# Attention block ends spread out and moved to GpSimd, clustering fold by fold: one layer pair on one core

## Chip, core and metric

The kernel runs on one core of one Trainium2 chip. The metric is the device time of one execution in microseconds (us); before the change the median of three runs is 4209.58 us, and they lie between 4209.54 and 4209.81.

The core's engines are named as in the profile: PE (TensorE, matrix products, and PEld its weight loads), DVE (VectorE), ACT (ScalarE), POOL (GpSimd), and SP, which issues the transfers.

## What is computed

Four images x of 256 channels by 64 x 64 points (4096 points) pass through two layers, all in 32-bit floats. The reference, cut to what matters:

```
# layer 0: attention over the 4096 points of an image
q = wq x + bq; k = wk x + bk                  # 32 channels each
attn = softmax(q^T k)                         # 4096 x 4096
v = wv x + bv                                 # 256 channels
x = gamma * (v attn^T) + x
# layer 1: clustering, then an MLP
n = group_norm(x)
feat = f_w n + f_b; val = v_w n + v_b         # 96 channels = 4 heads x 24
# each head, and each of the 2 x 2 folds of the picture (32 x 32 points):
cen, v_cen = 2 x 2 pooled feat, val           # 4 centres
sim = sigmoid(beta + alpha * <norm(cen), norm(feat)>)
sim = sim * one_hot(argmax over centres)
agg = (sim val + v_cen) / (count + 1)
out = sim^T agg                               # back to the points
y = x + ls1 * (proj_w out + proj_b)
y = y + ls2 * (w2 gelu(w1 group_norm(y)))
z = relu(bn(y * dw)); z = relu(bn(pw_w z))
```

## The kernel before

The images are worked on one after the other. An image's x stays in four SBUF tiles of 128 x 2 x 1024 (channels in two halves c, 1024 points each) and is overwritten in place by the attention's result, the clustering's and the MLP's. The order of the instructions on each engine is set by a scheduler from the program order and the buffers' release; a pool of n buffers makes the n+1st tile wait for the first one's last reader.

**Attention** (`attention`). Keys for all 4096 points and 16 pairs of value blocks (`v_pair`, L236) come first, together with the first scores. The 4096 query points form eight blocks (`nb`, 512 points each), and each block meets the keys in eight groups (`g`, 512 keys each): 64 units u. `score` (L266) computes a unit's scores into two PSUM halves (`halves`, two buffers in all), copies them into an SBUF slot `s` on ScalarE, and on VectorE takes the running maximum `top` (L286 from half 1, L289 from half 0). Scores run `LEAD` = 9 units ahead of their use, with 10 slots. When a block's eight units are scored, `fold`, `across` and `spread` make its maximum `mb`; `exps` (L318) then subtracts it on VectorE (L326), takes the exponential on ScalarE (L329) and sums the slots into `acc` on GpSimd (L331, L334), for all units whose turn the scheduler finds. `weigh` (L336) accumulates v times the exponentials into `av` (two PSUM banks, four quarters of a unit, 16 passes on TensorE). A block ends in `finish` (L347): `av` times gamma into `ts`, the denominator `den` (a product of ones with both halves of `acc`), its reciprocal `rden` (L356), a product (L358), the addition of the scaled v bias `gbv` and of x in one instruction (L360), and the statistics for the next norm (L363, `bn_stats`). `acc` has one buffer, so the next block's first sum waits for `den`.

**Clustering** (`cluster`). The first norm, `feat` and `val` (L436, L448), then squares on GpSimd (L504), point norms `nrm` and products with the centres `dots` (L510). `sg` holds the similarities of 128 points by 32 chunks by 16 (head, centre) pairs; `oh` is the one-hot choice. The four folds q are laid side by side in strips of 32: `sim` and `sgp` (with the pooling weights added) are 128 x 8 x 4 x 32, so that `agg` (L565) is computed in strips of 32 output partitions, `g` holds the projected centres of the four folds in four strips of 32 partitions (row 16 of each strip carries proj_b, through `projb` and `row16`), and the output product `op` (L626) uses 32-row strips into four banks. One VectorE instruction per piece then adds ls1 times it into x (L638), and `bn_stats` follows (L646).

**MLP** (`mlp`). The second norm, two matrix products with gelu between, and the last 1x1 convolution; its small tiles `hs` and `o` share the pool tag "w", as do `ts` and `sg`.

At the start, `projb` is made by two small products `pb_p` (L165) that need the transfer `pc_s`; they stand ahead of the first keys on TensorE. SP issues the transfers in program order, x's eight pieces first, then wv_s, bv_s, pc_s and the rest.

Of the kernel before, what the change touches and what calls it, by code (L numbers as in the profile page):

```python
# [8 lines left out]
F32 = mybir.dt.float32  # L9
# [4 lines left out]
P = 128  # L14
# [31 lines left out]
def attention_then_cluster_block(  # L46
# [61 lines left out]
    bv_s = loaded("bv_s", bv.rearrange("(k p o) -> p k o", p=P, o=1), [P, KC, 1])  # L108
# [52 lines left out]

    projb = const.tile([1, C], F32, name="projb")
    pb_p = ps_m.tile([P, NB], F32, tag="m", name="pb_p")
    for k in range(KC):
        nc.tensor.matmul(  # L165
            pb_p[:1, k * P : (k + 1) * P], par("proj_b", k), ident, start=True, stop=True
        )
    nc.vector.tensor_copy(projb, pb_p[:1, :C])
    row16 = const.tile([1, 4, 32], F32, name="row16")
    nc.gpsimd.memset(row16, 0.0)  # L170
    nc.gpsimd.memset(row16[:, :, 16:17], 1.0)

    gbv = const.tile([P, KC], F32, name="gbv")
    nc.vector.tensor_scalar(
        gbv, bv_s.rearrange("p k o -> p (k o)"), pv_s[:, PV["gamma"] : PV["gamma"] + 1], None, ALU.mult
    )
# [33 lines left out]
    def attention(b, xs):  # L210
# [25 lines left out]
        def v_pair(i):  # L236
            ps = ps_m.tile([P, 2, C], F32, tag="m", name=f"vp_{b}_{i}")
            for j in range(2):
                o = ((2 * i + j) * P) % XT
                for k in range(KC):  # L240
                    nc.tensor.matmul(  # L241
                        ps[:, j, :],
                        xs[(2 * i + j) * P // XT][:, k, o : o + P],
                        wv_s[:, k, :],
                        start=(k == 0),
                        stop=(k == KC - 1),
                    )
            if i % 2:
                nc.scalar.copy(v_t[:, 2 * i : 2 * i + 2, :], ps)
            else:  # L250
                nc.vector.tensor_copy(v_t[:, 2 * i : 2 * i + 2, :], ps)
# [44 lines left out]
        def across(nb):  # L296
            top = tops.pop(nb)
            tp = ps_m.tile([P, 4, P], F32, tag="m", name=f"tt_{b}_{nb}")
            for j in range(4):
                nc.tensor.transpose(tp[:, j, :], top[:, 0, j * P : (j + 1) * P], ident)  # L300
            mx = small.tile([P, 4], F32, tag="mx", name=f"mx_{b}_{nb}")
            nc.vector.tensor_reduce(mx, tp, AX.X, ALU.max)
            dg = work.tile([P, 4, P], F32, tag="dg", bufs=1, name=f"dg_{b}_{nb}")
            nc.vector.tensor_tensor(
                dg,
                ident.unsqueeze(1).to_broadcast([P, 4, P]),
                mx.unsqueeze(2).to_broadcast([P, 4, P]),
                ALU.mult,
            )
            return dg  # L310
# [36 lines left out]
        def finish(nb, av):  # L347
            acc = accs.pop(nb)
            ts = [work.tile([P, NB], F32, tag="w", bufs=5, name=f"t_{b}_{nb}_{c}") for c in range(KC)]
            nc.scalar.activation(ts[0], av[0], AF.Identity, scale=pvc("gamma"))  # L350
            nc.vector.tensor_scalar(ts[1], av[1], pvc("gamma"), None, ALU.mult)
            den = ps_m.tile([P, NB], F32, tag="m", name=f"den_{b}_{nb}")
            for t in range(2):
                nc.tensor.matmul(den, ones, acc[:, t, :], start=(t == 0), stop=(t == 1))
            rden = work.tile([P, NB], F32, tag="rden", bufs=1, name=f"rden_{b}_{nb}")
            nc.vector.reciprocal(rden, den)  # L356
            for c in range(KC):
                nc.vector.tensor_tensor(ts[c], ts[c], rden, ALU.mult)  # L358
                yb = block(xs, c, nb)
                nc.vector.scalar_tensor_tensor(  # L360
                    yb, ts[c], gbv[:, c : c + 1], yb, ALU.add, ALU.add
                )
                nc.vector.bn_stats(stats[:, 2 * nb + c, :], yb)  # L363
# [18 lines left out]
        av = None  # L382
        for u in range(units):
# [17 lines left out]
            weigh(u, av, 1)  # L401
            weigh(u, av, 2)
# [5 lines left out]
            if g == GRP - 1:  # L408
                finish(nb, av)
# [7 lines left out]
    def cluster(b, ys, stats):  # L417
# [99 lines left out]
        prn = work.tile([P, P], F32, tag="q", name=f"prn_{b}")  # L517
# [8 lines left out]
        sg = work.tile([P, NB], F32, tag="w", bufs=5, name=f"sg_{b}")  # L526
# [14 lines left out]
        nc.vector.tensor_tensor(quad(oh), quad(oh), over_m(best), ALU.is_equal)  # L541

        sim = spool.tile([P, 8, 4, 32], F32, tag="s", name=f"sim_{b}")
        sgp = spool.tile([P, 8, 4, 32], F32, tag="s", name=f"sgp_{b}")
        nc.gpsimd.memset(sim[:, :, :, 16:], 0.0)
        nc.gpsimd.memset(sim[:, :, :, 16:17], 1.0)
        nc.gpsimd.memset(sgp[:, :, :, 16:], 0.0)

        def folded(t):
            return t.rearrange("p (q j s) -> p q j s", q=4, j=8)  # L550

        for q in range(4):
            nc.vector.tensor_tensor(
                sim[:, :, q, :16], folded(sg)[:, q], folded(oh)[:, q], ALU.mult
            )

            nc.vector.tensor_tensor(
                sgp[:, :, q, :16], sim[:, :, q, :16], folded(pool_w)[:, q], ALU.add
            )


        agg_p = ps_m.tile([P, NB], F32, tag="m", name=f"agg_{b}")
        for j in range(8):
            for q in range(4):
                nc.tensor.matmul(  # L565
                    agg_p[q * 32 : (q + 1) * 32, :ED],
                    sgp[:, j, q, :],
                    val[q // 2][:, q % 2, j, :],
                    start=(j == 0),
                    stop=(j == 7),  # L570
                )
        cnt_p = ps_m.tile([P, NB], F32, tag="m", name=f"cnt_{b}")
        nc.tensor.matmul(cnt_p[:ED], ones[:, :ED], oh, start=True, stop=True)
        sums = work.tile([P, ED], F32, tag="q", name=f"sums_{b}")
        nc.scalar.copy(sums, agg_p[:, :ED])
# [12 lines left out]
        aggt = ps_m.tile([P, NB], F32, tag="m", name=f"aggt_{b}")  # L588
        nc.tensor.transpose(aggt[:ED, :P], sums, ident)
        agg = work.tile([P, 4, 32], F32, tag="q", name=f"aggs_{b}")  # L590
        nc.gpsimd.memset(agg, 0.0)
        nc.vector.tensor_tensor(
            agg[:ED, :, :16],
            aggt[:ED, :P].rearrange("p (q s) -> p q s", q=4)[:, :, :16],
            rc[:ED].rearrange("p (q s) -> p q s", q=4),
            ALU.mult,
        )

        gp = ps_m.tile([P, NB], F32, tag="m", name=f"gp_{b}")
        nc.tensor.matmul(  # L600
            gp[:, :C], agg[:ED].rearrange("p q s -> p (q s)"), wproj_s, start=True, stop=False
        )
        nc.tensor.matmul(gp[:, :C], row16.rearrange("p q s -> p (q s)"), projb, start=False, stop=True)
        g_s = work.tile([P, C], F32, tag="acc", bufs=1, name=f"g_{b}")
        nc.scalar.copy(g_s, gp[:, :C])

        sim_t = spool.tile([P, 2, NB], F32, tag="s", name=f"simt_{b}")
        for hb in range(2):
            tp = ps_m.tile([P, NB], F32, tag="m", name=f"tp_{b}_{hb}")
            for j in range(4):  # L610
                nc.tensor.transpose(
                    tp[:, j * P : (j + 1) * P],
                    sim[:, 4 * hb + j].rearrange("p q s -> p (q s)"),
                    ident,
                )
            nc.scalar.copy(sim_t[:, hb], tp)
        stats2 = small.tile([P, 2 * NBLK, 6], F32, tag="stats", name=f"st2_{b}")
        for hb in range(2):
            for c in range(KC):
                ops = [  # L620
                    ps_s.tile([P, 2, NB], F32, tag="s", name=f"op_{b}_{hb}_{c}_{f}")
                    for f in range(2)
                ]
                for q in range(4):
                    rows = slice(q * 32, (q + 1) * 32)
                    nc.tensor.matmul(  # L626
                        ops[q // 2][:, q % 2, :],
                        g_s[rows, c * P : (c + 1) * P],
                        sim_t[rows, hb, :],
                        start=True,  # L630
                        stop=True,
                    )
                for q in range(4):
                    fh, fw = q // 2, q % 2
# [3 lines left out]
                    nc.vector.scalar_tensor_tensor(  # L638
                        yq,
                        ops[fh][:, fw, :].rearrange("p (h w) -> p h w", h=16),  # L640
                        par("ls1", c),
                        yq,
                        ALU.mult,
                        ALU.add,
# [5 lines left out]
    def mlp(b, ys, stats2):  # L650
        ga, gb = group_norm(b, "gn2", stats2)
        ob = out[b].rearrange("(k p) h w -> p k (h w)", p=P)
        for nb in range(NBLK):
# [25 lines left out]
            for j in range(HID // P):  # L679
# [9 lines left out]
                h_s = work.tile([P, NB], F32, tag="w", bufs=5, name=f"hs_{b}_{nb}_{j}")  # L689
# [16 lines left out]
            for c in range(KC):  # L706
# [9 lines left out]
                o_s = work.tile([P, NB], F32, tag="w", bufs=5, name=f"o_{b}_{nb}_{c}")  # L716
# [88 lines left out]
```

## Time and profile before

| what | value |
|---|---|
| median of three runs | 4209.58 us |
| the profiled execution: time, span | 4209.54 us, 4207.7 us |
| mean granted TensorE clock | 0.929 of full |
| PE, PEld busy | 92%, 41% |
| DVE, ACT, POOL busy | 46%, 35%, 29% |
| one block of attention, end to end | about 81 us |
| clustering of one image, 710 to 811 us | PE clock 0.69 |

The profile is one execution. Its first part gives each engine's busy time; a busy PE is not PE at its peak, since matrix products overlap and their ends are modelled. The chain of waits follows the end of the span back to what released each step. The list of waits has, for each pair of instructions, the idle time of the waiting engine in total, how often, and the longest. A group of instructions is shown as line, engine, operation, written tile <- read tiles, shapes, count, then busy time, mean ns of one, and the idle time in front of it with what ended it. A timeline row is start, duration, engine, line, operation, count, and in brackets the idle time before it. A matrix product of 32-bit floats shows as two passes.

### The profile page before, as it was taken

The page shows a single profiled execution, that of the slowest core. Times are in us where ns is not written, and L with a number is a line of the kernel's source. Part 1 is how long each engine was busy: PE and PEld are TensorE (multiplying, and loading weights), DVE is VectorE, ACT ScalarE, POOL GpSimd, SP SyncE. Part 2 cuts the span into 40 slices and gives each one's busy share as a digit, 9 for nine tenths or more (in the row PEclk, how much of TensorE's full clock was granted, in tenths as well). Part 3 has the DMA queues.
Part 4 walks back from the last instruction along what each step waited for, and adds up shares of the span by engine and source line. Part 5 has one row for each costly group of instructions (what it writes and reads, how often), then busy time and mean ns, then how long its engine had stood idle before and what let it go on. Part 6 is the DMA issues. An engine that isn't in the chain of part 4 may idle for free.

```text
span 4207.7 us, 28649 instructions
## 1 busy us (share of the span) xinstructions
PE 3864.4 (92%) x11176; PEld 1736.7 (41%) x11176; DVE 1950.2 (46%) x1982; ACT 1471.3 (35%) x1723; POOL 1202.3 (29%) x526
## 2 busy tenths in 40 slices
PE   8998998799999899889999989988999989998899
PEld 4333334544433333444443333344444333335444
DVE  4557655400456765540055675643005576564300
ACT  5434432122634443212263443411226344341122
POOL 1534533000143553300024454340003345343000
PEclk9999999699999999969999999996999999998799
DMA  2000000010000000001000000000100000000000
GB/s 75 1 0 0 0 0 0 1 38 28 15 1 0 0 0 0 0 1 40 25 16 0 0 0 0 0 1 5 35 25 16 0 0 0 0 0 1 5 15 20
DMA packets 17639, 38.99 MB, mean 9 GB/s; under 512 B 2688, under 2 KB 4832, under 8 KB 17504
## 3 DMA queue, kind: packets, MB, share of 16 engines
q1 hardware_dynamic: 17504, 37.16, 2.5%
q8 instruction: 88, 1.44, 0.1%
q14 instruction: 47, 0.39, 0.0%
HBM read 20.38 MB, written 16.78 MB: 9 GB/s over the span
## 4 chain that ended last, share of the span: by engine, by line
PE 81%; DVE 16%; issue 2%; ACT 1%; DMA 0%; SPq 0%; DVEq 0%; ACTq 0%
PE av L339 37%; PE h L682 11%; PE mo L671 10%; PE sc L276 7%; DVE s L326 3%; DVE x L360 3%; PE pw L709 3%; PE vp L241 3%; DVE rden L356 2%; DVE t L358 2%; PE qp L256 2%; PE kp L220 1%; PE dots L510 1%; PE fp L436 1%; PE vp L448 1%
## 5 line engine op out<-in xcount | busy, mean ns | idle before, releaser
L339 PE MATMUL av<-s,v 128*128 128x512 f32 x4096 | 1877.7, 612 | 0.0
L339 PEld LDWEIGHTS av<-s,v 128*128 128x128 f32 x4096 | 780.7, 196 | 1076.4 <-issue 1054.2
L334 POOL TENSOR_TENSOR acc<-acc,s 128x1024 f32<-128x1024 f32 x448 | 1090.6, 2434 | 163.8 <-ACT s L329 130.8
L331 POOL TENSOR_TENSOR acc<-s 128x1024 f32<-128x1024 f32 x32 | 75.5, 2360 | 2207.6 <-ACT s L329 1168.5
L329 ACT ACTIVATE s<-s 128x1024 f32<-128x1024 f32 x512 | 532.0, 1056 | 444.6 <-DVE s L326 430.1
L326 DVE TENSOR_TENSOR s<-s,mb 128x1024 f32<-128x1024 f32 x512 | 591.1, 1210 | 36.2 <-PE mb L314 36.2
L286 DVE TENSOR_TENSOR top<-sc,top 128x1024 f32<-128x1024 f32 x224 | 272.1, 1215 | 677.4 <-PE sc L276 677.4
L276 PE MATMUL sc<-q,k 32*128 32x512 f32 x2048 | 356.2, 666 | 178.0 <-DVE top L289 171.2
L282 ACT COPY s<-sc 128x1024 f32<-128x1024 f32 x256 | 258.0, 1008 | 681.6 <-PE sc L276 681.6
L682 PE MATMUL h<-xn,w_s 128*128 128x512 f32 x1024 | 488.1, 601 | 8.3 <-DVE xn L656 6.2
L671 PE MATMUL mo<-hs,w_s 128*128 128x512 f32 x1024 | 476.1, 593 | 0.0
L698 DVE SCALAR_TENSOR_TENSOR x<-mo,pc_s,x 128x512 f32<-128x512 f32 x64 | 48.0, 751 | 918.5 <-PE mo L671 915.1
L690 ACT ACTIVATE hs<-h,pv_s 128x512 f32<-128x512 f32 x256 | 175.9, 687 | 579.2 <-PE h L682 577.0
L287 ACT COPY s<-sc 128x1024 f32<-128x1024 f32 x256 | 258.5, 1010 | 135.2 <-DVE top L286 93.6
L682 PEld LDWEIGHTS h<-xn,w_s 128*128 128x128 f32 x1024 | 197.5, 193 | 255.2 <-issue 253.2
L671 PEld LDWEIGHTS mo<-hs,w_s 128*128 128x128 f32 x1024 | 194.9, 190 | 244.8 <-issue 244.8
L289 DVE TENSOR_TENSOR top<-sc,top 128x1024 f32<-128x1024 f32 x224 | 273.4, 1220 | 17.9 <-DVE top L286 0.5
L276 PEld LDWEIGHTS sc<-q,k 32*128 32x128 f32 x2048 | 95.4, 190 | 384.8 <-DVE top L289 191.1
L360 DVE SCALAR_TENSOR_TENSOR x<-t,gbv,x 128x512 f32<-128x512 f32 x64 | 161.6, 2564 | 0.0
L709 PE MATMUL pw<-z,wpw_s 128*128 128x512 f32 x256 | 118.7, 607 | 3.3 <-ACT z L702 3.3
L241 PE MATMUL vp<-wv_s,x 128*128 128x256 f32 x512 | 119.1, 386 | 0.0
L284 DVE TENSOR_TENSOR top<-sc,s 128x1024 f32<-128x1024 f32 x32 | 39.2, 1224 | 158.6 <-ACT s L282 158.6
(143 smaller groups left out, 1972.8 us busy)
## 6 DMA issues: line engine op xcount, KB each, us to landing
x<-in_x SPq DMA_DIRECT2D x32, 512.0 KB, 4.8
out<-o SPq DMA_DIRECT2D x64, 256.0 KB, 2.0
w_s<-in_w SPq DMA_DIRECT2D x2, 1024.0 KB, 6.8
cst<-in_consts SPq DMA_DIRECT2D x1, 338.0 KB, 7.4
wqk_l<-in_wqk SPq DMA_DIRECT2D x1, 256.0 KB, 2.7
wv_s<-in_wv SPq DMA_DIRECT2D x1, 256.0 KB, 10.0
wpw_s<-in_wpw SPq DMA_DIRECT2D x1, 256.0 KB, 8.1
wfv_s<-in_wfv SPq DMA_DIRECT2D x1, 192.0 KB, 6.6
```

The costliest lines, as they stand in the source:

```text
L276: nc.tensor.matmul(halves[r // 2][:, r % 2, :], k_s[rows, g, :], q_s[rows, :], start=True, stop=True)
L282: nc.scalar.copy(s[:, 0:2, :], halves[0])
L286: nc.vector.tensor_tensor(top, halves[1], top, ALU.max)
L287: nc.scalar.copy(s[:, 2:4, :], halves[1])
L289: nc.vector.tensor_tensor(top, halves[0], top, ALU.max)
L326: nc.vector.tensor_tensor(sh, sh, mxs[nb].unsqueeze(1).to_broadcast([P, 2, NB]), ALU.subtract)
L329: nc.scalar.activation(sh, sh, AF.Exp)
L334: nc.gpsimd.tensor_tensor(acc, acc, s[:, 2 * h : 2 * h + 2], ALU.add)
L339: nc.tensor.matmul(av[c], v_t[:, RG * g + quarter, c * P : (c + 1) * P], slots[u][:, quarter, :], start=(g == 0 and quarter == 0), stop=(g ...
L360: nc.vector.scalar_tensor_tensor(yb, ts[c], gbv[:, c : c + 1], yb, ALU.add, ALU.add)
L671: nc.tensor.matmul(acc[c], w2_s[:, j, c * P : (c + 1) * P], hs[j], start=(j == 0), stop=(j == HID // P - 1),)
L682: nc.tensor.matmul(ps[:, 0, :], w1_s[:, k, j * P : (j + 1) * P], xn[:, k, :], start=(k == 0), stop=(k == KC - 1),)
```

## The change

In `finish`, the two halves of `acc` are first summed on GpSimd, the denominator is one product and is copied to SBUF on ScalarE, and its reciprocal is taken in four pieces, handed back to the loop as a list `later`, one of which is run in each of the next block's units; the fifth entry scales `t_s` by the reciprocal and adds it into x, both on GpSimd for both channel halves at once, and takes the statistics on VectorE. v's bias is added to v itself on GpSimd, after a copy that is now always ScalarE's. In `cluster`, the side-by-side layout goes: `sim` is a plain 128 x 512 tile, `agg` is computed with the values as stationary operand in 32 products of 16 columns, the projection is one product for each fold, and the output is made fold by fold: four transposes, a copy, two products, a scaling with bias on ScalarE and an addition on VectorE. The set-up of `projb`, `row16` and `gbv` goes, and pool sizes change a little.

```diff
-    bv_s = loaded("bv_s", bv.rearrange("(k p o) -> p k o", p=P, o=1), [P, KC, 1])
+    bv_s = loaded("bv_s", bv.partition_broadcast(P), [P, C])
...
-    for k in range(KC):
-        nc.tensor.matmul(
-            pb_p[:1, k * P : (k + 1) * P], par("proj_b", k), ident, start=True, stop=True
-        )
-    nc.vector.tensor_copy(projb, pb_p[:1, :C])
...
+    lsb = const.tile([P, KC], F32, name="lsb")
+    nc.vector.tensor_tensor(lsb, par("ls1"), par("proj_b"), ALU.mult)
...
-            if i % 2:
-                nc.scalar.copy(v_t[:, 2 * i : 2 * i + 2, :], ps)
-            else:
-                nc.vector.tensor_copy(v_t[:, 2 * i : 2 * i + 2, :], ps)
+            pair = v_t[:, 2 * i : 2 * i + 2, :]
+            nc.scalar.copy(pair, ps)
+            nc.gpsimd.tensor_tensor(
+                pair, pair, bv_s.unsqueeze(1).to_broadcast([P, 2, C]), ALU.add
+            )
...
         def finish(nb, av):
+
             acc = accs.pop(nb)
-            ts = [work.tile([P, NB], F32, tag="w", bufs=5, name=f"t_{b}_{nb}_{c}") for c in range(KC)]
-            nc.scalar.activation(ts[0], av[0], AF.Identity, scale=pvc("gamma"))
-            nc.vector.tensor_scalar(ts[1], av[1], pvc("gamma"), None, ALU.mult)
+            t_s = work.tile([P, KC, NB], F32, tag="t", bufs=1, name=f"t_{b}_{nb}")
+            nc.scalar.activation(t_s[:, 0], av[0], AF.Identity, scale=pvc("gamma"))
+            nc.vector.tensor_scalar(t_s[:, 1], av[1], pvc("gamma"), None, ALU.mult)
+            nc.gpsimd.tensor_tensor(acc[:, 0], acc[:, 0], acc[:, 1], ALU.add)
             den = ps_m.tile([P, NB], F32, tag="m", name=f"den_{b}_{nb}")
-            for t in range(2):
-                nc.tensor.matmul(den, ones, acc[:, t, :], start=(t == 0), stop=(t == 1))
+            nc.tensor.matmul(den, ones, acc[:, 0], start=True, stop=True)
             rden = work.tile([P, NB], F32, tag="rden", bufs=1, name=f"rden_{b}_{nb}")
-            nc.vector.reciprocal(rden, den)
-            for c in range(KC):
-                nc.vector.tensor_tensor(ts[c], ts[c], rden, ALU.mult)
-                yb = block(xs, c, nb)
-                nc.vector.scalar_tensor_tensor(
-                    yb, ts[c], gbv[:, c : c + 1], yb, ALU.add, ALU.add
-                )
-                nc.vector.bn_stats(stats[:, 2 * nb + c, :], yb)
+            nc.scalar.copy(rden, den)
+
+            def piece(i):
+                r = rden[:, i * P : (i + 1) * P]
+                nc.vector.reciprocal(r, r)
+
+            def last():
+                nc.gpsimd.tensor_tensor(
+                    t_s, t_s, rden.unsqueeze(1).to_broadcast([P, KC, NB]), ALU.mult
+                )
+                o = (nb % 2) * NB
+                yb = xs[nb // 2][:, :, o : o + NB]
+                nc.gpsimd.tensor_tensor(yb, yb, t_s, ALU.add)
+                for c in range(KC):
+                    nc.vector.bn_stats(stats[:, 2 * nb + c, :], yb[:, c, :])
+
+            return [lambda i=i: piece(i) for i in range(4)] + [last]
...
             weigh(u, av, 1)
+            if g and later:
+                later.pop(0)()
             weigh(u, av, 2)
...
             if g == GRP - 1:
-                finish(nb, av)
+                later = finish(nb, av)
+        for piece in later:
+            piece()
...
+        sim = work.tile([P, NB], F32, tag="top", bufs=1, name=f"sim_{b}")
+        nc.vector.tensor_tensor(sim, sg, oh, ALU.mult)
+
+        nc.vector.tensor_tensor(sg, sim, pool_w, ALU.add)
...
+        agg_p = ps_m.tile([P, NB], F32, tag="m", name=f"agg_{b}")
+        for ch in range(32):
+            q = ch // 8
+            nc.tensor.matmul(
+                agg_p[:ED, q * 16 : (q + 1) * 16],
+                val[q // 2][:, q % 2, ch % 8, :],
+                sg[:, ch * 16 : (ch + 1) * 16],
+                start=(ch % 8 == 0),
+                stop=(ch % 8 == 7),
+            )
...
+        g_s = work.tile([16, 4, C], F32, tag="acc", bufs=1, name=f"g_{b}")
+        for qq in range(2):
+            gp = ps_m.tile([P, 2, C], F32, tag="m", name=f"gp_{b}_{qq}")
+            for t in range(2):
+                q = 2 * qq + t
+                nc.tensor.matmul(
+                    gp[:16, t, :],
+                    agg[:ED, q * 16 : (q + 1) * 16],
+                    wproj_s,
+                    start=True,
+                    stop=True,
+                )
+            nc.scalar.copy(g_s[:, 2 * qq : 2 * qq + 2, :], gp[:16])
...
+        for q in range(4):
+            fh, fw = q // 2, q % 2
+            for hb in range(2):
+                tp = ps_m.tile([P, NB], F32, tag="m", name=f"tp_{b}_{q}_{hb}")
+                for j in range(4):
+                    ch = q * 8 + hb * 4 + j
+                    nc.tensor.transpose(
+                        tp[:16, j * P : (j + 1) * P], sim[:, ch * 16 : (ch + 1) * 16], ident
+                    )
+                sim_t = work.tile([16, NB], F32, tag="w", bufs=4, name=f"simt_{b}_{q}_{hb}")
+                nc.scalar.copy(sim_t, tp[:16])
+                for c in range(KC):
+                    op = ps_m.tile([P, NB], F32, tag="m", name=f"op_{b}_{q}_{hb}_{c}")
+                    nc.tensor.matmul(
+                        op, g_s[:, q, c * P : (c + 1) * P], sim_t, start=True, stop=True
+                    )
+                    t_s = work.tile([P, NB], F32, tag="w", bufs=4, name=f"cl_{b}_{q}_{hb}_{c}")
+                    nc.scalar.activation(
+                        t_s, op, AF.Identity, scale=par("ls1", c), bias=lsb[:, c : c + 1]
+                    )
+                    yq = ys[2 * fh + hb][:, c, :].rearrange("p (h f w) -> p f h w", h=16, f=2)[
+                        :, fw
+                    ]
+                    nc.vector.tensor_tensor(
+                        yq, t_s.rearrange("p (h w) -> p h w", h=16), yq, ALU.add
+                    )
+                    nc.vector.bn_stats(stats2[:, 4 * q + 2 * hb + c, :], yq)
```

The removed clustering code is that of L543 to L646 in the functions above, from `sim` and `sgp` to the output.

## The prediction

> **What bounds the kernel now.** I read the chain of waits first: it is 81% TensorE and 16% VectorE, so TensorE's order carries the time, and what matters is where VectorE cuts in. The list of waits names that place, and a third row is a one-off at the start.
>
> ```profile
> PE 81%; DVE 16%; issue 2%; ACT 1%; DMA 0%; SPq 0%; DVEq 0%; ACTq 0%
> ...
> POOL acc L331 <- PE den L354: 1039.1, 28, 39.0
> ...
> PE sc L276 <- DVE top L289: 171.2, 24, 7.2
> ...
> PE pb_p L165 <- DMA pc_s<-in_pc: 18.3, 1, 18.3
> ```
>
> TensorE's scores wait for VectorE's `top` maximum 24 times, 7.1 us each: six per image, the ends of query blocks 0 to 5 (later ends have no scores to compute). GpSimd is idle some 38 us before each block's first sum. The timeline at the end of block 1 of the first image shows who sits in front of that `top`:
>
> ```profile
> 239.44 3.35 DVE L356 RECIPROCAL rden<-den 128x512 f32<-128x512 f32 x1
> ...
> 243.79 3.43 DVE L358 TENSOR_TENSOR t<-t,rden 128x512 f32<-128x512 f32 x2
> ...
> 247.15 5.57 DVE L360 SCALAR_TENSOR_TENSOR x<-t,gbv,x 128x512 f32<-128x512 f32 x2
> 252.64 1.27 DVE L363 BATCH_NORM_STATS2 st<-x 128x6 f32<-128x512 f32 x2
> 253.83 1.20 DVE L289 TENSOR_TENSOR top<-sc,top 128x1024 f32<-128x1024 f32 x1
> ...
> 255.09 2.08 PE L276 MATMUL sc<-q,k 32*128 32x512 f32 x4 [7.15 <-DVE top L289]
> ...
> 257.10 9.48 PE L339 MATMUL av<-s,v 128*128 128x512 f32 x16
> ```
>
> The scores due at 246.8 run at 255.1, and the next 16 products take 9.48 us instead of the usual 7.06: the granted clock has fallen. Blocks without the stall would take about 70 us (8 steps of 8.14 plus small matmuls); GpSimd's first sums are 81.4 apart (238.92 and 320.30). So a stalled end costs about 11.3 us: 8.0 of stall, 3.3 of slow clock.
>
> ```profile
> 238.92 2.36 POOL L331 TENSOR_TENSOR acc<-s 128x1024 f32<-128x1024 f32 x1 [38.04 <-PE den L354]
> 241.36 10.81 POOL L334 TENSOR_TENSOR acc<-acc,s 128x1024 f32<-128x1024 f32 x4
> 257.39 24.29 POOL L334 TENSOR_TENSOR acc<-acc,s 128x1024 f32<-128x1024 f32 x10 [5.23 <-ACT s L329]
> ```
>
> After a block's end GpSimd runs a burst of 15 sums, 2.43 us each (24.29 over 10).
>
> [...] a pair of L360 takes 5.57 us beside GpSimd's sums and 1.41 at the end of the last block, where GpSimd is idle. [...] here 2.43 us for 1024 elements, against 0.69 us for 512 (L304) on VectorE. [...] half speed lasts 4.7 us behind a stall (a 128x512 pass 0.85 us, against 0.43).
>
> **The change at the block ends.** VectorE loses L358 and L360, 9.0 us here; its reciprocal (3.35) becomes four of 128x128, 0.95 each (the row of `prn`), spread out. GpSimd gains a half sum (about 1.2 us, ahead of the block's end, inside the 38 idle us), a product and a sum over 128x1024, 2.43 each. ScalarE gains a copy of the denominator (0.59, as L249), beside other work. The denominator is two passes fewer on TensorE: 0.86 us.
>
> I step through block 1's end with the built order of the changed kernel, numbering scores by unit. Denominator done 237.9; `rden` copied 238.7. VectorE, from 238.3 on: subtraction, reciprocal, subtraction, `top` of unit 25, subtraction, second `top`, done about 245.1, in time for scores 26 at 246.0: the old stall is gone. Then reciprocal, two subtractions, reciprocal, two subtractions, `top`, reciprocal, `top`: 254.8, so scores 27 (due 254.1) lose 0.7. Two more subtractions: 257.1. Next on VectorE are the two `bn_stats`, and these now **wait for GpSimd's addition into x**. GpSimd starts at 238.06 and has in front of it, in its order, the sums of units 16 to 21: 2.44 + 10 x 2.43, to 264.8, then product and addition, to **269.7**. VectorE stands 12.6 us. Behind it are the last two subtractions (units 23), whose exponentials stand in ScalarE's queue ahead of the copies of scores 27, and both `top` of scores 27; TensorE's scores 28 need these halves free. 269.7 + 1.3 (bn) + 2.3 + 2.6 = 275.9, with the second copy 276.2. TensorE was ready at 263.0: a new stall of 13 us, longer than the old, with the same slow clock behind it. Before, 255.09 was the stalled scores 26; now 276.2 is scores 28, two steps (16.3) further: 276.2 - 255.1 - 16.3 = +4.8 a block end (the shorter denominator is inside). 24 x 4.8 = **+115**. Bounds: a pitch of 2.37 without gaps makes it +4.0; if the reciprocals hold GpSimd up for all of their 3.8 us, +8.6. I take no hold-up[...].
>
> Blocks 6: no scores, 4 x -0.86 = **-3**. Last end of each image: all is serial. Before, from denominator to `bn_stats` 696.5 to 704.4. Now copy 0.6 + 4 reciprocals 3.7 + 2 x 2.43 on GpSimd in place of 3.4 + 1.3 + 1.4: +2.6 each, **+10**.
>
> v's bias: 16 GpSimd sums of 128x512 per image, about 1.2 us, and 8 more copies on ScalarE. In that stage TensorE sets a 4.72 us step; ScalarE gets 2 x 1.01 + 2 x 0.59 = 3.2 and GpSimd is idle: nothing. bv_s grows from 1 KB to 128 KB on SP's queue, ahead of pc_s (18.3), which ScalarE needs ahead of the sixth keys' copies, due near 20 us; bv_s itself is first needed near 32: nothing, at most the 0.3 us that 128 KB take at x's rate.
>
> **The start.** Without `pb_p`, TensorE's first keys no longer wait behind pc_s (18.3) but only for x's first tile, whose landings SP's issues show (7.8 and 9.0). Keys start near 9 instead of 19.3; the x tiles land 1.3 us per transfer, faster than 16 us of key work: **-10**.
>
> **Clustering.** Before, the tail from `oh` (778.6) to the second norm (811.0) is 32.4 us and VectorE-bound: 16 x (0.70 + 0.60) of it.
>
> ```profile
> L510 PE MATMUL dots<-cbd,feat 96*128 96x16 f32 x256 | 55.3, 375 | 6.0 <-DVE cbd L491 6.0
> ...
> L626 PE MATMUL op<-simt,g 32*128 32x512 f32 x128 | 57.3, 1116 | 15.8 <-DVE x L638 15.8
> ...
> L565 PE MATMUL agg<-val,sgp 128*32 128x96 f32 x256 | 12.6, 349 | 26.1 <-DVE sgp L557 26.1
> ```
>
> Now: `sim`, `sg` 1.4 (before 1.6). `cnt` 1.7. The sums become 32 calls of 16 columns, 64 passes, in the shape of `dots`, whose 64 passes per image take 13.85 (0.216 a pass): with weights of 96 columns for 128 I take 0.16, so 10.2 (high end 13.8) against some 3 before. Four projections and two copies: about 5. First output matmul near 796.7. Then eight rounds: four transposes into one of two PSUM buffers, ScalarE copies, two matmuls of two passes, ScalarE scales each (0.68), VectorE adds and takes statistics. With two buffers a round is a chain: at half clock matmul 1.7[...], next matmul, transposes 0.85, copy 0.58 behind a 0.68: 5.4 us; at full clock 3.6. VectorE needs 2.7, so it no longer sets the pace. Tail end: 840 at half clock, 826 at full: +29 or +15 an image. At half clock TensorE streams 60 to 80% of a round; in the same stage before, some 70% left the clock at half, while solid work raised it, so I expect it to alternate: +22, 4 x 22 = **+88** (ends 59 and 117).
>
> w's buffers 5 to 4: output stores land in 2.1 us, their buffers are wanted again over 5 us later: nothing. SP's queue order is the same.
>
> **Sum.** 115 - 3 + 10 - 10 + 88 = +200 on the profiled execution's 4209.54 (span 4207.7; the median 4209.58 is the same): **4410 us**.
>
> **Rivals.** (1) Faster: GpSimd finishes its addition before VectorE arrives, at 257.1 instead of 269.7. Then no long stall is left: 11.3 - 0.7 + 0.9 = 11.5 off each end, 24 x -11.5 = -276, sum -276 - 3 + 10 - 10 + 88 = -191, **4019**. It decides where the new stall is 200/24 = 8.3 us shorter: addition done at 261.4, a pitch of 1.75 us. For it: 38 us of idle GpSimd. Against: that idle time lies at the block's other end, and no row is below 2.34. 9%. (2) Clustering stays VectorE-paced: clock full, cost near +10 an image, **4362**; 15%. (3) Half clock throughout and the sums at `dots`' price, +33 an image: **4454**; 18%. (4) Gains and losses cancel within 0.2%: 3%. The main forecast has 55%, itself 4365 to 4455.
>
> **Range and chances.** The unknowns of the block ends (+96 to +206) and of clustering (+59 to +117) do not all fall to one side; 4340 to 4480 takes in rivals 2 and 3 and leaves out rival 1. A measurement tells 0.2% from no change. Faster 9%, same 3%, slower 88%.
>
> **What would show it.** In the changed profile: VectorE's `bn_stats` waiting some 12 us for GpSimd's addition to x, 24 times; TensorE's scores waiting for `top` 24 times at 12 to 13 us; GpSimd's two new rows near 2.4 us; first keys near 9 us; the sums `agg` near 10 us an image; ScalarE's copy between transposes and output matmuls on the chain. I am wrong if `bn_stats` waits little, or if clustering, 101 us from first `fp` work to the second norm (710 to 811), takes no longer.

## The result, and the profile after

| what | before | after |
|---|---|---|
| median | 4209.69 us of 4 runs (4209.54 to 4210.3) | 4400.35 us of 4 runs (4399.13 to 4401.84) |
| profiled execution: span | 4207.7 us | 4400.0 us |
| mean granted TensorE clock | 0.929 | 0.905 |

The kernel became slower: the ratio of the times is 1.0453, with a 95% interval of 1.0435 to 1.0471. The predicted time was 4410 us in a range of 4340 to 4480.

The chain of waits of the changed kernel, by engine. TensorE had 81% of it and GpSimd nothing; now GpSimd is on the path:

```profile
PE 71%; POOL 12%; DVE 10%; ACT 4%; issue 2%; DMA 0%; POOLq 0%; SPq 0%; ACTq 0%
```

The list of waits of the changed kernel (who waited, for whom: us in total, how often, the longest). The row of scores waiting for `top` is gone, and two new ones stand in its place; 24 of the 28 waits in the second are block ends, of 13.5 to 13.8 us each:

```profile
DVE st L358 <- POOL x L356: 405.6, 32, 16.7
...
PE sc L263 <- ACT s L274: 330.5, 28, 13.8
```

The timeline at the end of block 1 of the first image, the place that was shown of before (start, duration, engine, line, and in brackets the idle time before):

```profile
248.80 2.34 DVE L313 TENSOR_TENSOR s<-s,mb 128x1024 f32<-128x1024 f32 x2
...
259.70 2.34 POOL L351 TENSOR_TENSOR t<-t,rden 128x1024 f32<-128x1024 f32 x1
262.12 2.34 POOL L356 TENSOR_TENSOR x<-x,t 128x1024 f32<-128x1024 f32 x1
...
264.48 1.29 DVE L358 BATCH_NORM_STATS2 st<-x 128x6 f32<-128x512 f32 x2 [13.35 <-POOL x L356]
265.69 2.33 DVE L313 TENSOR_TENSOR s<-s,mb 128x1024 f32<-128x1024 f32 x2
...
267.94 1.22 DVE L273 TENSOR_TENSOR top<-sc,top 128x1024 f32<-128x1024 f32 x1
...
269.74 1.00 ACT L274 COPY s<-sc 128x1024 f32<-128x1024 f32 x1
270.79 2.09 PE L263 MATMUL sc<-q,k 32*128 32x512 f32 x8 [13.60 <-ACT s L274]
```

Read from the bottom: TensorE's scores 28 wait 13.60 us for a PSUM half. ScalarE empties it at 269.74, behind an exponential that needs the subtraction of 265.69; that subtraction and the maximum `top` stand on VectorE behind `bn_stats`; and `bn_stats` waited 13.35 us for GpSimd's addition, which came behind ten sums. Three engines stand still because a statistics instruction, whose result the next norm needs only some 450 us later, is next in VectorE's order.

The clustering's output of the changed kernel, one round of its timeline (each of the other late rounds looks the same):

```profile
821.98 1.02 PE L595 MATMUL tp<-ident,sim 128*16 128x128 f32 x4
...
823.03 0.57 ACT L599 COPY simt<-tp 16x512 f32<-16x512 f32 x1 [0.17 <-PE tp L595]
...
823.66 3.78 PE L602 MATMUL op<-simt,g 16*128 16x512 f32 x4 [0.66 <-ACT simt L599]
...
827.48 0.78 ACT L606 ACTIVATE cl<-op,lsb,pc_s 128x512 f32<-128x512 f32 x1 [0.93 <-PE op L602]
```

A round takes 5.39 us, and a product's four passes 3.78. The windows of that stretch (us, busy time of PE, PEld, DVE, ACT and POOL, then the granted clock) say why: half clock (0.50), though TensorE is busy 84% of the time. e10 to e12 show where the half clock comes from.

```profile
817.00:821.00 4.00, 3.34 (x7) 1.27 (x5) 1.60 (x3) 1.67 (x3) 0.00 (x0) 0.50 0.00 0
821.00:825.00 4.00, 3.34 (x8) 1.19 (x7) 2.77 (x4) 1.51 (x3) 0.00 (x0) 0.50 0.00 0
```

The new groups, by line (busy time, mean ns of one):

```profile
L351 POOL TENSOR_TENSOR t<-t,rden 128x1024 f32<-128x1024 f32 x32 | 74.8, 2338 | 70.6 <-DVE rden L348 70.6
L356 POOL TENSOR_TENSOR x<-x,t 128x1024 f32<-128x1024 f32 x32 | 74.8, 2338 | 2.2
...
L565 PE MATMUL agg<-sg,val 128*96 128x16 f32 x256 | 41.3, 320 | 0.0
```

Where the 192.3 us between the two spans lie, from the starts of the same instructions in both timelines, all four images:

| stage | predicted | measured |
|---|---|---|
| start, up to the first sum of block 0 of the first image | -10 | -9.4 |
| seven block ends of each image (first sum of block 0 to that of block 7) | +115 - 3 | +95.5 |
| last end of each image (to the first norm) | +10 | +8.4 |
| clustering, from `fp` to the one-hot choice `oh` | 0 | -13.5 |
| clustering, from `oh` to the second norm | +88 | +109.2 |
| the rest (values, MLP, changes of image) | 0 | +2.1 |

### The profile page after: what moved, and what is told of

It is laid out like the page before. It is cut to its first block, busy times and chain, and to the rows that moved or that the text cites. A ratio compares the mean times of both kernels' runs of the same rounds, so it can differ in the third digit from the quotient of the medians.

```text
span 4400.0 us, 28969 instructions
## 1 busy us (share of the span) xinstructions
PE 3904.1 (89%) x11216; PEld 1761.0 (40%) x11216; DVE 1682.5 (38%) x1893; ACT 1577.7 (36%) x1876; POOL 1433.7 (33%) x668
## 4 chain that ended last, share of the span: by engine, by line
PE 71%; POOL 12%; DVE 10%; ACT 4%; issue 2%; DMA 0%; POOLq 0%; SPq 0%; ACTq 0%
PE av L326 28%; PE h L651 10%; PE mo L640 10%; POOL acc L321 9%; PE sc L263 5%; DVE s L313 5%; PE pw L678 3%; PE vp L227 3%; PE op L602 3%; POOL x L356 1%; POOL t L351 1%; PE qp L243 1%; PE kp L206 1%; PE fp L437 1%; PE dots L511 1%
## 5 line engine op out<-in xcount | busy, mean ns | idle before, releaser
L321 POOL TENSOR_TENSOR acc<-acc,s 128x1024 f32<-128x1024 f32 x448 | 1057.0, 2359 | 32.6
L263 PE MATMUL sc<-q,k 32*128 32x512 f32 x2048 | 328.6, 689 | 332.6 <-ACT s L274 330.5
L236 POOL TENSOR_TENSOR v<-v,bv_s 128x512 f32<-128x512 f32 x64 | 82.2, 1290 | 1196.7 <-ACT v L235 1195.9
L358 DVE BATCH_NORM_STATS2 st<-x 128x6 f32<-128x512 f32 x64 | 41.2, 685 | 405.6 <-POOL x L356 405.6
L602 PE MATMUL op<-simt,g 16*128 16x512 f32 x128 | 113.7, 1036 | 21.4 <-ACT simt L599 21.4
```

The costliest lines, as they stand in the source:

```text
L263: nc.tensor.matmul(halves[r // 2][:, r % 2, :], k_s[rows, g, :], q_s[rows, :], start=True, stop=True)
L321: nc.gpsimd.tensor_tensor(acc, acc, s[:, 2 * h : 2 * h + 2], ALU.add)
```

## The experiments

Two theories were to be tested. For the attention: the order on VectorE, with `bn_stats` ahead of work that is due, costs the time; the rivals were the additional work on GpSimd itself, and VectorE's time. For the clustering: the chain through two buffers at half clock; the rivals were VectorE's pace and the sums alone. The table gives the stages of the second image in each kernel, in us: "block" is the distance of the first sums of blocks 2 and 3, "front" goes from the first `fp` to the last `oh` instruction, "tail" from there to the second norm. In e3 the tail of the other three images is 62.3.

| kernel | median | block | front | tail |
|---|---|---|---|---|
| before | 4209 | 81.4 | 67.4 | 32.7 |
| after | 4400.4 | 85.2 | 64.0 | 60.1 |
| e1 ends only | 4299.6 | 85.5 | 64.0 | 31.9 |
| e2 clustering only | 4318.9 | 81.4 | 67.4 | 62.4 |
| e3 late statistics | 4027.4 | 69.0 | 67.1 | 60.0 |
| e4 ends of e3, old clustering | 3907.1 | 69.0 | 67.2 | 32.7 |
| e5 statistics two scores earlier | 4062.0 | 70.3 | 64.1 | 62.3 |
| e7 ends on VectorE | 4167.7 | 74.9 | 67.4 | 62.3 |
| e6, e8, e10 output in other buffers | 4440.1, 4379.2, 4346.3 | 85.1 to 85.5 | 64.0 | 68.6, 55.4, 46.9 |
| e11, e12 with 128 rows | 4331.2, 4344.5 | 85.1, 85.3 | 64.0 | 43.8, 46.4 |

### e1 and e2: each half alone

```diff
 e1: after, with
-        sim = work.tile(...)            # clustering fold by fold
+        sim = spool.tile(...)           # clustering of before, projb and row16 at the start
 e2: before, with the clustering of after, lsb, and no pb_p at the start
```

Expected of e1:

> The changed block ends and v bias with the clustering and the start of the kernel before (to make room in SBUF, prn and best take slots of other tiles and the statistics have one buffer). Theory (the two parts add up, each at the size that the traces show by stage): the block ends cost +95, the last ends +9, the value stage -4, so 4310 us, between 4300 and 4320, with bn_stats waiting some 12 us for the addition 24 times. Rival A (the loss sits in the clustering, the ends are about even): near 4215. Rival B (the parts hide each other, so that neither alone shows its share): above 4330 or below 4290 without fitting A.

Expected of e2:

> The changed clustering and start with the block ends, gbv and v copies of the kernel before. Theory: the start gives -9, the clustering +96 (24 an image), so 4296 us, between 4285 and 4305; the rounds of the output at 5.4 us and half clock. Rival A (the loss sits here): 4390. Rival B (only the slower sums count, the rounds keep VectorE's pace): some 4230.

e1 took 4299.6 us (ratio 1.0218, 1.0201 to 1.0235), just under its expected range, e2 4318.9 (1.0262, 1.0247 to 1.0277). Both halves lose, 90 and 110 us; the rivals that put the loss into one of them fall. e2 missed its expectation by 23 us, because its tail is 62.4, not 60.1 (no round at full clock; after has one), and its front is 67.4, not 64.0. The front runs the same instructions in all these kernels and takes 64 or 67.4; in before `nrm` takes 11.85 us at a mean granted clock of 0.59, and in after 9.72 at 0.73, so the difference goes with the clock.

The clock records of the traces show more. In all 14 traces the clock is either 0.50 or 1.00, and every stretch between its first and its last change lasts a whole multiple of 3.41 us (82 such stretches in before, 80 in after): within each of these traces the changes lie on a fixed grid. The windows around them (columns as above), first before, where the front begins at 710.5, then after, where it begins at 727.2:

```profile
714.00:717.00 3.00, 2.81 (x17) 2.61 (x15) 0.09 (x1) 0.68 (x1) 0.00 (x0) 0.69 0.00 0
744.00:747.00 3.00, 3.00 (x28) 3.00 (x27) 2.82 (x4) 0.00 (x0) 3.00 (x2) 0.93 0.02 5
...
730.00:733.00 3.00, 2.36 (x18) 1.92 (x16) 0.60 (x3) 0.68 (x1) 0.00 (x0) 0.97 0.00 0
764.00:767.00 3.00, 3.00 (x18) 3.00 (x17) 0.00 (x0) 0.00 (x0) 0.00 (x0) 0.55 0.00 0
```

In before the clock rises 5.3 us after the front's first product and stays up for nine steps of the grid (30.7 us), in after it rises 3.0 us after it and stays up for ten (34.1). All 56 fronts (four images of 14 kernels) are of one of these two kinds: the clock up within 3.0 to 4.3 us and then ten steps, which makes 64.0 us, or within 5.0 to 5.8 us and then nine, which makes 67.1 to 68.0. So a front's length goes with the place of its first product on the grid, which shifts with everything that runs earlier and at which the change does not aim. The one fast round is such a step too: in after's tail the clock is up for 3.4 us, in e2's not at all.

### e3, e4 and e5: the place of bn_stats

```diff
+                if nb and p % GRP == 5:     # e5: == 3
+                    nc.vector.tensor_copy(
+                        stats[:, 2 * nb - 2 : 2 * nb, 0:1], tops[p // GRP][:, 0, 0:2].unsqueeze(2)
+                    )
...
-                for c in range(KC):
-                    nc.vector.bn_stats(stats[:, 2 * nb + c, :], yb[:, c, :])
-            return [lambda i=i: piece(i) for i in range(4)] + [last]
+            return [lambda i=i: piece(i) for i in range(4)] + [last, tally]   # tally: the two bn_stats
```

The copy writes where `bn_stats` will write, and reads the maximum behind which it is to stand: it holds the place, since the scheduler moves an instruction forward otherwise. Expected of e3:

> The changed kernel with one thing moved: the bn_stats of a block stand on VectorE behind the maximum of the sixth scores of the block two further on (scores 29 for block 1; a copy of two columns holds them there, 0.1 us each), when GpSimd's addition is done. All the work stays. Theory (it is the position of bn_stats in VectorE's order, ahead of the last subtractions and of the maxima, that costs): the waits of 12.6 us go and blocks take about 68 to 70 us in place of 85.2, 24 x -15.5, so about 4030 us, between 3995 and 4070. Rival A (GpSimd's additional work[...] is the cost, bn_stats only sees it): 4350 or more. Rival B (another wait takes its place, as long as the old one of 7.1 us with its slow clock, blocks of 80): near 4280.

Expected of e4:

> The changed block ends with the late bn_stats, the clustering of the kernel before, and its pb_p moved from the start to the first image's clustering. Theory: e3 less the 96 us of the clustering, so about 3930 us, between 3895 and 3975, faster than both kernels by over 6%. Rival (the stall of the block ends comes back in another form): 4180 or more.

Expected of e5:

> As e3, but bn_stats stand behind the maximum of the fourth scores (27 for block 1), two scores earlier. In e3 VectorE was done with that maximum at 238.5 us and GpSimd's addition at 246.4, so bn_stats wait here about 7 us, 24 times, with only the maxima of scores 28 behind them. Theory (a wait costs what stands behind it and is due: the halves of scores 28 come free at 250.2, scores 29 are due at 248.8): a stall of about 1.4 us an end, so 4027 + 24 x 1.4 = 4060 us, between 4035 and 4110. Rival (VectorE's time is the limit and each us of its wait is lost): 4027 + 24 x 7 = 4195.

e3 took 4027.4 us (0.9571, 0.9557 to 0.9585): moving two small instructions (and adding the copy that holds their place, 0.7 to 0.9 us here, not the 0.1 expected) takes 373 us off the changed kernel and brings it below the kernel before, with all of GpSimd's additional work in place. The rival that blamed this work falls. In e3's list of waits only the eight late ends (blocks 6 and 7) are left in this row:

```profile
DVE st L362 <- POOL x L356: 81.3, 8, 15.6
```

The timeline of e3 at the same block end shows scores 28 on time, the addition, scores 29, and the statistics after them:

```profile
238.98 1.14 PE L263 MATMUL sc<-q,k 32*128 32x512 f32 x8
...
244.01 2.34 POOL L356 TENSOR_TENSOR x<-x,t 128x1024 f32<-128x1024 f32 x1
...
248.84 1.14 PE L263 MATMUL sc<-q,k 32*128 32x512 f32 x8
...
253.65 1.29 DVE L362 BATCH_NORM_STATS2 st<-x 128x6 f32<-128x512 f32 x2
```

e5 is the sharper test, since it keeps a wait of VectorE and only changes what stands behind it. Its timeline:

```profile
240.43 1.14 PE L263 MATMUL sc<-q,k 32*128 32x512 f32 x8
...
247.82 1.29 DVE L362 BATCH_NORM_STATS2 st<-x 128x6 f32<-128x512 f32 x2 [7.15 <-POOL x L356]
...
251.32 1.41 PE L263 MATMUL sc<-q,k 32*128 32x512 f32 x8 [0.97 <-ACT s L274]
```

VectorE waits 7.15 us at each of the 24 ends, and TensorE loses 0.97 of it here, about as much at the other ends except the sixth of each image, and 2.7 at that one: 31 us in all for VectorE's 172. The time is 4062.0 us (0.9652, 0.9638 to 0.9667), where 4060 was expected and 4195 if each us of VectorE's wait counted. That the 4060 is so close is in part luck: by the stages, block ends cost 44 us more than in e3, not 34, and the four fronts, by their clock, 12 less. The main reading stands: a wait costs what is due behind it.

e4 puts e3's ends together with the old clustering and the start without `pb_p`: 3907.1 us (0.9283, 0.9269 to 0.9297). It beats both kernels. Its chain of waits is TensorE almost throughout:

```profile
PE 94%; DVE 5%; ACT 1%; POOL 0%; issue 0%; DMA 0%; SPq 0%; DVEq 0%; ACTq 0%; POOLq 0%
```

### e7: the same ends, but on VectorE

```diff
-                nc.gpsimd.tensor_tensor(t_s, t_s, rden..., ALU.mult)
+                nc.vector.tensor_tensor(t_s, t_s, rden..., ALU.mult)
...
-                nc.gpsimd.tensor_tensor(yb, yb, t_s, ALU.add)
+                nc.vector.tensor_tensor(yb, yb, t_s, ALU.add)
```

> The changed kernel with product and addition into x on VectorE in place of GpSimd, at the same places of the program, bn_stats behind them as in the change: only the engine is undone, the pieces of the reciprocal stay. VectorE's order puts product, addition and statistics among the last subtractions, ahead of the maximum of scores 27. Theory (in an unstalled block, as e3 shows, the maximum of scores 27 is over 0.5 us before scores 28 are due, so some 8 to 10 us more on VectorE ahead of it stall TensorE by about 8 and drop its clock): blocks of 80, near 4290 us, between 4230 and 4330. Rival (spreading the reciprocal was enough; the engine does not matter): near 4050. Rival 2 (as bad as the change[...]): 4400.

It took 4167.7 us (0.9903, 0.9886 to 0.9919): none of the three values, and outside the range of the first. Its timeline in the same place:

```profile
238.18 2.38 DVE L351 TENSOR_TENSOR t<-t,rden 128x1024 f32<-128x1024 f32 x1
...
241.62 2.26 DVE L356 TENSOR_TENSOR x<-x,t 128x1024 f32<-128x1024 f32 x1
...
247.84 1.94 PE L263 MATMUL sc<-q,k 32*128 32x512 f32 x8 [3.59 <-ACT s L274]
```

The mechanism was as expected (scores 28 late, behind the maximum), the size was not. Beside GpSimd's sums product and addition, now two instructions in place of four, take 2.38 and 2.26 us, not the 9.0 that L358 and L360 took before, and the stall is 3.59. So the changed kernel's move to GpSimd, with the statistics where they were, lost 233 us against this version; with the statistics out of the way (e3) it gained 140. The move to GpSimd alone does not make the kernel slow; with this order it does. e3 and e7 differ in the place of the statistics as well: ends on VectorE with late statistics were not run, so what the engine alone is worth stays open.

### e9: the start alone

```diff
-    pb_p = ps_m.tile(...)      # and its products, at the start
+        if b == 0:             # the same, in the first image's clustering
```

> The kernel before with one thing moved: the two products pb_p and their copy from the start to the first image's clustering. Theory: the first keys begin near 7.6 instead of 19.3 us, the first block's sum 9 us earlier, and all of it stays: 4200 us, between 4198 and 4203. Rival (the transfers of x or ScalarE's table hold the keys up by as much later on): 4209.

4202.0 us (0.9982, 0.9974 to 0.999): the keys begin at 7.63 instead of 19.26 us, and most of the gain stays.

### e6, e8, e10, e11 and e12: what makes a round long

e6 and e8 changed the buffers, e8 and e10 also put the transposes first:

```diff
 e6
-                    op = ps_m.tile([P, NB], F32, tag="m", ...)
+                    op = op2[:, c]          # op2: one ps_s tile of two banks for both c
 e8: op as in e6, and all transposes with their copies (sim_ts) in a loop ahead of the outputs
 e10: as e8, but
+                    op = ps_m.tile(...) if c else ps_s.tile(...)[:, 0]
 e11: as e10, e12: as after, both with
-        g_s = work.tile([16, 4, C], ...)
+        g_s = work.tile([P, 4, C], ...)     # zeroed first; sim_ts 128 rows high and zeroed too
```

Expected of e6, e8 and e10, in this order:

> The changed kernel with the output products op in the four banks that the scores use in the attention (two buffers of two banks, one for both channel halves), the transposes alone in the two old buffers. Same work. Theory (a round of 5.4 us is a chain through two buffers: TensorE waits in it for ScalarE): the chain breaks, the round falls to TensorE's own work at half clock, 4.8 us, or, if the clock then rises, towards VectorE's 2.8: between 4400 - 4 x 7 x 0.6 = 4383 and 4400 - 4 x 7 x 2.6 = 4327; I take 4340, since TensorE would be busy without a gap. Rival (the half clock does not depend on the gaps): 4383. Rival 2 (ScalarE or VectorE sets the round anyhow): 4400, no change.

> After e6, in which ScalarE's order put each copy of transposes behind the scaling of the round before: the changed kernel with the transposes of all eight rounds and their copies ahead of the first half of the output products (eight parts of two of the attention's slots in place of four small buffers), and op in the four banks. Same work. Theory (the round of 5.4 us is a chain TensorE, ScalarE, TensorE, with TensorE idle in it for want of data): TensorE runs ahead; at half clock its own 8 x 1.02 + 32 x 0.85 = 35 us set the output stage in place of 42, at full clock VectorE's 16 x 1.42 = 23 us. So 4400 - 4 x 7 = 4372 to 4400 - 4 x 18 = 4328; since TensorE then has no gaps I expect the clock to rise after some us: 4340. Rival (half clock stays for TensorE's narrow operands whatever the gaps): 4372. Rival 2 (the chain is not what sets it): 4400.

> As e8, but each output product has a bank of its own among four buffers (in e8 a buffer of two banks came free only when both halves were scaled, and TensorE still idled 0.87 us in each 4.65 us, at half clock, after having run the first products and transposes without a gap at full clock). Same work. Theory (the gaps keep the clock at half): without them it rises and VectorE's 1.42 us a product sets the pace, so the output stage ends near 830 instead of 842.7: 4379 - 4 x 12 = 4331, or, if it alternates, 4344. Rival (half clock whatever the gaps, TensorE solid at 1.7 us a product): 4 x 8.7 less, 4344 at best with the clock at 0.50 all through. Rival 2 (it waits for ScalarE as before): 4379.

e6 took 4440.1 us (1.0548, 1.0532 to 1.0564), 40 more than the change and none of the expected values: ScalarE's order now put each copy of transposes behind the second scaling of the round before, so the buffers were free and the chain became longer, 6.35 us a round. It says nothing about the clock. e8 took 4379.2 (1.0402, 1.0386 to 1.0419), with late rounds of 4.65 us and 0.87 us of idle TensorE in each, still at half clock; the nearest value was the rival's 4372. e10 took 4346.3 (1.0324, 1.0306 to 1.0343), near the rival's 4344, and its windows contradict the theory that the gaps hold the clock down. TensorE is busy without a gap. While transposes, which read 128 rows, stand between the products the clock is 1.00; from 814.9 on the products run alone, and at 818.1 it falls:

```profile
811.00:815.00 4.00, 4.00 (x20) 1.68 (x19) 1.39 (x2) 2.18 (x6) 0.00 (x0) 1.00 0.00 0
815.00:819.00 4.00, 3.99 (x8) 1.50 (x9) 2.18 (x4) 3.52 (x6) 0.00 (x0) 0.88 0.00 0
819.00:823.00 4.00, 4.00 (x6) 1.66 (x5) 4.00 (x8) 2.11 (x4) 0.00 (x0) 0.50 0.00 0
823.00:827.00 4.00, 4.00 (x6) 1.40 (x6) 4.00 (x7) 2.14 (x3) 0.00 (x0) 0.50 0.01 2
```

What was left were the 16 rows that each product uses. e11 and e12 fill them up to 128 with zeros, which leaves the result, the number of passes and their columns as they are:

> As e10, in which TensorE ran 23 products without a gap at a granted clock of 0.50 (a pass of 0.85 us). One thing changed: g and the transposed similarities are 128 rows high in place of 16, the other 112 filled with zeros by GpSimd beforehand, so each output product has the same passes and columns but uses all 128 rows. Theory (TensorE busy with 16 rows does not count as busy enough for the clock): the clock stays at 1.00, a pass takes 0.43, VectorE sets the pace, which it almost did in e10: 2 us an image less, 4338, and the clock of the stage is the verdict. Rival (the clock falls for another reason, such as zeros or the waits of the stage before): 0.50 and 4346 as in e10.

> The changed kernel with the same filling up to 128 rows and nothing else (order of the stage, two buffers and chain as they are). Theory (16 rows hold the clock at half): rounds of 3.6 us in place of 5.4, 4400 - 4 x 7 x 1.8 = 4350, clock near 1 in the stage; if the gaps of the chain hold it down too, it alternates, about 4375. Rival (rows do not matter): 4400.

e11 took 4331.2 us (1.0292, 1.0275 to 1.0309) with the clock at 1.00 while TensorE worked on the products, and nothing but the rows is changed from e10. e12, which is the changed kernel but for the rows and the slots that hold the transposed similarities, took 4344.5 (1.0323, 1.0308 to 1.0339), where 4350 was expected. e12's windows in the stretch shown above of after:

```profile
815.00:819.00 4.00, 3.28 (x11) 1.15 (x9) 3.17 (x5) 2.45 (x4) 0.00 (x0) 1.00 0.00 0
819.00:823.00 4.00, 3.26 (x12) 1.21 (x12) 2.98 (x5) 2.62 (x5) 0.00 (x0) 1.00 0.00 0
```

TensorE has more gaps than in e10 and works at full clock. A round takes 3.31 us (814.09 to 817.40), the 3.30 of after's one round at full clock, and the mean duration by line falls from 1036 ns in after to 619:

```profile
L606 PE MATMUL op<-simt,g 128*128 128x512 f32 x128 | 63.5, 619 | 22.8 <-ACT simt L603 22.8
```

So of the 27.4 us by which the second image's tail grew in the change (32.7 to 60.1), 13.7 are the half clock of the products with 16 rows (60.1 to 46.4). The other 13.7 are there at full clock too; the sums `agg` alone, 10.3 us of TensorE for 3.2, are 7 of them.

## Why the prediction was right, and where its steps were off

The time (4410 for 4400) and the side were right, and both large costs, the block ends and the output of the clustering, came about in the way described. That the time was so close is luck: the seven block distances came out 16.5 us below the forecast and the fronts 13.5 below, the tails 21 above, and these cancel for the most part.

- **GpSimd's lateness.** From its first sum to the addition's end 31.6 us were predicted (238.06 to 269.7), and 31.5 measured (232.93 to 264.46). `bn_stats` waits 13.35 us for 12.6, scores 28 stall 13.60 for 13. That the release comes through ScalarE's second copy was in the working too.
- **The price of an end.** Predicted +4.8, measured +3.5 to +5.2, in the mean +4.15 for the six ends, and -0.95 for the block without one. The mis-sized term is "the same slow clock behind it": at the end shown the 16 products behind the stall take 8.81 us, not 9.48 as before, since the clock is up again 5.4 us after the restart, in before 6.8 us after it (the 4.7 of the working counts from the products, not from the scores ahead of them). The spread is this clock too. From a block's first sum to the restart it is 16.16 us in before and 37.82 in after, within 0.1 at all 24 ends; that makes 37.82 - 16.16 - 16.28 - 0.86 = +4.5 for every end. But the half clock behind the restart lasts 4.3 to 7.6 us in before and 5.2 to 5.7 in after, depending on where the restart falls on the grid, and a pass takes 0.85 us in it for 0.43, so half of such time is lost: with half of the difference of the two added, the six ends come to +4.1 in the mean. The loss of 0.7 at scores 27 did not appear. This makes +95.5 for +112.
- **No hold-up by the reciprocals.** Taken as nothing, an estimate of the author's, and nothing was there: GpSimd's ten sums take 24.36 us (24.29 before).
- **Last ends, start, v's bias.** +8.4 for +10 (the terms that the working names add up to +3.1 an image, not to its +2.6; measured +2.1), -9.4 for -10 (e9 alone: -7.6), and no visible share of v's bias: from the first keys to the first sum of images 2 to 4 it is 1 us less in all.
- **The sums `agg`.** 10.3 us an image for 10.2, and the first output matmul comes 17.7 us after the choice `oh` is done (18.1 in the working).
- **The clock in the rounds: wrong.** The step "solid work raised it, so I expect it to alternate" failed. Both pitches were about right (5.4 at half clock: 5.39; 3.6 at full: 3.30), but seven of eight rounds ran at half clock, and the tail cost +27.3 an image instead of +22; e2 shows +29.7, the value that the text had given for half clock. e10 shows that solid work of this kind does not raise the clock (4.00 of 4.00 us busy at 0.50, 819 to 823), e11 and e12 that with 128 rows it is up (1.00 in the same window). The working counted on 60 to 80% for a round and some 70% in before; within before's output TensorE was busy for 2.57 of 3.00 us (798 to 801), more than in a round, and the clock stood at 0.50 all the same. That clustering came out at +95.7 for +88 is owed to the front, 3.4 us shorter, which no step foresaw: ten steps of the clock's grid at full speed instead of nine.
- **The rivals.** Rival 1 (no long stall left, 4019) did not happen but exists: e3, at 4027, is the changed kernel with its condition met from the other side, VectorE arriving late instead of GpSimd early. Rival 2 (VectorE's pace) falls with the timeline of the rounds. Rival 3's half clock came true, its dearer sums did not.

## What to carry to other kernels

Before moving work to an idle engine, ask when its result is ready and which instruction takes it, and then what stands behind that instruction in its engine's order: a result that nobody needs soon must be taken late, behind everything that is due. Look at the order the scheduler produced, not at the place in the program, and hold the place with a dependence if need be. Where products use few rows and the granted clock is low, try filling them up with zeros (here 16 rows to 128: the clock went from 0.50 to 1.00, a round from 5.39 to 3.31 us).

## What the hardware showed unexpectedly

- **The clock follows more than TensorE's occupation.** Products with 16 rows ran without a gap for 16 us at 0.50 (e10, 0.85 us a pass), and the same passes with 128 rows, 112 of them zeros, at 1.00 with gaps of a fifth of the time (e12). The rows of one product are not all of it. The first window below is before's output, where four products of 32 rows each work in four strips and TensorE is busy for 86% of the time; the second is `dots` in after, with 96 rows but only 16 columns a pass and no gap. Both stay at 0.50:

```profile
798.00:801.00 3.00, 2.57 (x8) 0.54 (x4) 3.00 (x6) 0.00 (x0) 0.00 (x0) 0.50 0.00 0
...
776.00:779.00 3.00, 3.00 (x15) 3.00 (x16) 0.00 (x0) 0.00 (x0) 0.00 (x0) 0.50 0.00 0
```

  Which numbers of rows between 16 and 128 are enough, and for how many columns, was not tried.
- **Beside GpSimd's sums these instructions of VectorE take longer, and not by one factor.** In e7 the addition over 1024 elements takes 2.25 us beside the sums and 1.23 at the last end, where GpSimd is idle; in before L360 over 512 takes 2.82 and 0.75. The form alone does not decide it: of before's two L358 at a block's end, the same instruction on the same shape, the first takes 0.68 us and the second 2.84. At the end of block 1 the first begins at 243.79, just ahead of a sum, and this sum takes 2.88 us instead of 2.36; the second begins at 244.39, inside the sum, which ends at 246.68, and is done 0.5 us later. GpSimd's sums beside e7's work come every 2.56 us instead of 2.43.
